# Two row groups for the distance products, and convolution products that leave their result channel by channel

## The chip, the cores and the metric

The kernel runs on one core of one Trainium2 chip. The metric is the device time of one execution in microseconds. The engines are named as the profile names them: PE (TensorE matmul), PEld (TensorE weight load), DVE (VectorE), ACT (ScalarE), POOL (GpSimd), SP (SyncE, which here only issues DMAs).

## The reference, cut to what matters

64 graphs of 256 nodes with 256 features go through two layers, all in float32. The first layer has two branches that meet in a GRU cell. One is a convolution over the nodes, a 1x1 and then a 17-tap one, both with batch norm. The other sends messages weighted by exp(-distance) times the adjacency matrix, with distances between nodes in a learned space of 3 dimensions.

```
xc = transpose(x)                                   # channels by nodes
h = relu(bn1(conv1d(xc, conv1_w)))
h = bn2(conv1d(h, conv2_w, pad 8))                  # 17 taps
x_conv = transpose(relu(h + xc))
s = x @ w_se.T + b_se                               # 3 coordinates per node
sq = sum(s * s)
dist = sq[n] + sq[m] - 2 * (s @ s.T)
A = exp(-dist) * adj
x_nmp = A @ relu(x @ w_msg.T + b_msg)
gi = concat(x_conv, x_nmp) @ w_ih.T + b_ih ; gh = x @ w_hh.T + b_hh
r, z = sigmoid(gi_r + gh_r), sigmoid(gi_z + gh_z)
x1 = layernorm(x + (1 - z) * tanh(gi_n + r * gh_n) + z * x)
# layer 2
h = layernorm(x1)
x2 = layernorm(x1 + x1 + relu((adj @ h) @ W_rel + b_rel + h @ W_root))
```

## The kernel before, in words

The program is one written-out stream: the order in which the Python code issues instructions is the order on each of the five engine queues (`manual_schedule`), and each engine takes its queue in order. PE writes to PSUM, which is a pool of eight banks of 512 columns; every `bank(...)` call takes one, and the matmul that fills it waits for the last reader of the bank's former owner.

**The convolution** handles 8 graphs at a time (`BG`, 8 batches). The 256 nodes of a graph are cut into 16 residues of 16 places, so that the 17-tap filter becomes products of polynomials, which are split by butterflies on DVE into small leaves (`split_all`, `split_u`), multiplied on PE leaf by leaf (`products`, `last_products`, `product`) with 47 matrices of 256x256, and merged back on DVE (`merges` and the statements after `STAGE[b] = "inverse"`). All of it lives in one big tile `X` of 48 slots of 128 x 256; DVE's `stt` helper (L102) does most of the work. In a slot the partitions are channels and the 256 columns are two halves of channels times 128 places. `product` takes 128 columns of a slot as the stationary operand and 256 columns of a matrix as the moving one. So the result comes out with the places on the partitions and the output channels along the columns. The matrices of batch 0 are built in place (`W2[0]`); for later batches they are read from DRAM (`w2m`) into `w`.

After the merges the convolution adds the input x (`x_by_tiles`, loaded as `xb` in four pieces of 512 KB, a pool of two buffers that the next batch's first loads use as well) and turns the sum back to channels by places with PE transposes (`channels`, into `ps_xc`); ACT takes them to SBUF through a Relu into `xc`. The shift of the second batch norm is added along the rows in `last_products` (L419), from `bn2_row`, which `along_rows` makes at the start. The input turned to channels is also written to DRAM once per batch (`xt_dram`, in `conv`) and read back as `xT` by `load`.

**The graphs** go one by one through messages (`messages`), the turning of their 3 coordinates plus half a squared norm (`factors`: two transposes of 128 x 4 into `ps_sT`, two ACT copies into `lr`), the distances (`distances`: two matmuls with 4 rows each, both halves in one bank, then two Exp), the adjacency mask, the message sum (`passing`), the gates (`gates_rz`, `gates_n`), the update, and the second layer (`transposes_h`, `project`, `aggregate`). The loop over k mixes stages of graphs k-1 to k+3. Between the stages stand ten calls of `pump` per graph, which issue the next batch's convolution piece by piece: `conv` is a generator that yields an estimated cost after each piece, and a pump draws pieces until the share of the total that is due has been issued, or until the generator yields None. Batch 0 has no graphs beside it and stands at the start, with the filters.

Of the kernel before, what the change touches and what calls it, by code (L numbers as in the profile page):

```python
# [16 lines left out]
P = 128  # L17
B, N, D = 64, 256, 256
C = D // P
# [30 lines left out]
LEAVES += [(U + 4 + k, U + 6 + k, a) for k, a in enumerate(leaf_angles(PI / 2, 2))]  # L50
LEAVES += [(U + 2, U + 3, PI / 2)]
NM = 3 * len(LEAVES) + 2
OB = 7


# [19 lines left out]
def gnn_two_layers(  # L75
# [35 lines left out]
        eng.dma_start(out=t, in_=src.rearrange("(c p) n -> p c n", p=P))  # L111
        return t

    def x_by_tiles(b, q):

        t = conv_pool.tile([P, 4, D], F32, tag="xb", name="xb")
        nc.sync.dma_start(
            out=t, in_=x[b * BG:(b + 1) * BG].rearrange("g (t j) d -> (g t) j d", j=M)[:, 4 * q:4 * q + 4, :])
        return t


    chan_sb = const.tile([P, 8, C], F32)
    nc.scalar.dma_start(out=chan_sb, in_=chan)
# [12 lines left out]


    bn_scale, bn_shift = [], []
    bn2_row = const.tile([P, 2, D], F32)

    def batch_norms():
        for i in range(2):
# [10 lines left out]

    def along_rows(pool):

        for i, v in enumerate((bn_scale[1], bn_shift[1])):
            ps = bank("ps_row")
            for c in range(C):
                dg = pool.tile([P, P], F32, tag="dg", name="dg", bufs=4)
                nc.vector.tensor_scalar(dg, ident, v[:, c:c + 1], None, ALU.mult)  # L160
                nc.tensor.matmul(ps[:, c * P:(c + 1) * P], ones, dg, start=True, stop=True)
            nc.scalar.copy(bn2_row[:, i, :], ps[:, :D])


    w2m = tc.dram_tile([NM, C, P, D], F32, name="w2m")
# [2 lines left out]
    def filters(pool):  # L168
        W2[0] = pool.tile([P, C, NM, D], F32, name="w2all")
        pieces, groups = [], []  # L170
        for c in range(C):
            for o0, o1 in ((0, 12 * OB), (12 * OB, 24 * OB), (24 * OB, D)):
                starts = [min(o, D - OB) for o in range(o0, o1, OB)]
                for a in range(0, len(starts), 4):
                    groups.append((len(pieces), starts[a:a + 4]))
                pieces.append((c, o0, o1))
        WT = {}

        def fetch(i):
            if i < len(pieces):  # L180
                c, o0, o1 = pieces[i]
                WT[i] = pool.tile([P, TAPS, o1 - o0], F32, tag="wt", name="wt", bufs=2)
                nc.sync.dma_start(out=WT[i], in_=w2T[c, :, :, o0:o1])

        def scaled(i, starts):

            c, o0, o1 = pieces[i]
            ws = pool.tile([P, 4, TAPS, OB], F32, tag="ws", name="ws", bufs=3)
            n, o = len(starts), starts[0]
            nc.vector.tensor_mul(  # L190
                ws[:, :n], WT[i][:, :, o - o0:o - o0 + n * OB].rearrange("p k (b o) -> p b k o", o=OB),
                bn2_row[:, 0, o:o + n * OB].rearrange("p (b o) -> p b o", o=OB).unsqueeze(2)
                .to_broadcast([P, n, TAPS, OB]))
            return ws

        def turned(ws, n):
            ps = bank("ps_tT")
            for b in range(n):
                nc.tensor.transpose(ps[:TAPS * OB, b * P:(b + 1) * P], ws[:, b].rearrange("p k o -> p (k o)"), ident)
            tT = pool.tile([TAPS * OB, 4, P], F32, tag="tT", name="tT", bufs=2)  # L200
            nc.scalar.copy(tT[:, :n].rearrange("k b p -> k (b p)"), ps[:TAPS * OB, :n * P])
            return tT

        fetch(0)
        fetch(1)
        yield
        along_rows(pool)
        TT = {}
        WS = {0: scaled(*groups[0]), 1: scaled(*groups[1])}
        TT[0] = turned(WS[0], 4)  # L210
        for i, (piece, starts) in enumerate(groups):
            c = pieces[piece][0]
            if i + 2 < len(groups):
                WS[i + 2] = scaled(*groups[i + 2])
                if groups[i + 2][0] != groups[i + 1][0]:
                    fetch(groups[i + 2][0] + 1)
            if i + 1 < len(groups):
                TT[i + 1] = turned(WS[i + 1], len(groups[i + 1][1]))
            for a, o in enumerate(starts):
                ps = bank("ps_w")  # L220
                nc.tensor.matmul(ps[:, :NM * OB], TT[i][:, a, :], tap_sb, start=True, stop=True)
                skip = OB - D % OB if o == D - OB else 0
                pv = ps[:, :NM * OB].rearrange("p (f o) -> p f o", o=OB)
                nc.scalar.copy(W2[0][:, c, :, o + skip:o + OB], pv[:, :, skip:])
            if i + 1 == len(groups) or pieces[groups[i + 1][0]][0] != c:
                for f in range(0, NM, 8):
                    g = min(f + 8, NM)
                    nc.sync.dma_start(out=w2m[f:g, c].rearrange("f p o -> p f o"), in_=W2[0][:, c, f:g, :])
            yield
# [148 lines left out]
        return lambda m, c: t[:, m, c, :]  # L378

    def product(ps, slot, w, m):  # L380
        for c in range(C):
            nc.tensor.matmul(ps, X[:, slot, c * P:(c + 1) * P], w(m, c), start=(c == 0), stop=(c == C - 1))  # L382

    def products(b, first, sums):

# [16 lines left out]
    def last_products(b):  # L402
# [9 lines left out]

        def take():
            nc.scalar.copy(X[:, S2 + 6, :], p1[:, :D])
            nc.scalar.copy(X[:, U + 1, :], p3[:, D:])
            nc.vector.tensor_sub(X[:, U + 2, :], X[:, S2 + 6, :], p2[:, :D])
            nc.vector.tensor_add(X[:, U + 3, :], X[:, S2 + 6, :], p1[:, D:])

            nc.vector.tensor_add(X[:, U, :], p3[:, :D], bn2_row[:, 1, :])  # L419
        return take  # L420

    def conv(b):
# [97 lines left out]

        xcs = [work.tile([P, C, 4, N], F32, tag="xc", name="xc", bufs=3) for _ in range(2)]

        def channels(q):
            for o in range(C):
                ps = bank("ps_xc")
                for j in range(4):
                    nc.tensor.transpose(ps[:, j * P:(j + 1) * P], X[:, V + 4 * q + j, o * P:(o + 1) * P], ident)
                pv = ps.rearrange("p (j g t) -> p j g t", j=4, g=BG)
                for h in range(2):
                    nc.scalar.activation(  # L530
                        xcs[h][:, o].rearrange("p g (t j) -> p j g t", j=M)[:, 4 * q:4 * q + 4],
                        pv[:, :, 4 * h:4 * h + 4, :], AF.Relu)
                yield 1.0

        before = []
        for q in range(4):
            xb = x_by_tiles(b, q)
            nc.vector.tensor_add(sl(V + 4 * q, 4), sl(V + 4 * q, 4), xb)
            yield cost(4)
            yield None  # L540
            before.append(channels(q))
            if len(before) > 2:
                yield from before.pop(0)
        for c_ in before:
            yield None
            yield from c_
        for g in range(BG):
            XC[b * BG + g] = (xcs[g // 4], g % 4)

# [16 lines left out]

    def messages(k):
        MSG[k] = work.tile([P, C, D], F32, tag="msg", name="msg", bufs=3)
        st = work.tile([P, C, 4], F32, tag="st", name="st", bufs=3)
        for m in range(C):  # L570
            ps = bank("ps_msg")
            for c in range(C):
                nc.tensor.matmul(ps[:, :D + 4], XT[k][:, c, m * P:(m + 1) * P], wms[:, c, :],  # L573
                                 start=(c == 0), stop=(c == C - 1))
            nc.vector.tensor_add(st[:, m, 0:3], ps[:, D:D + 3], bse_row)
            nc.vector.tensor_add(MSG[k][:, m, :], ps[:, :D], bmsg)  # L576
        nc.scalar.activation(MSG[k], MSG[k], AF.Relu)  # L577

# [2 lines left out]
        nc.gpsimd.tensor_mul(sq, st[:, :, 0:3], st[:, :, 0:3])  # L581
        nc.gpsimd.tensor_add(ns, sq[:, :, 0], sq[:, :, 1])
        nc.gpsimd.tensor_add(ns, ns, sq[:, :, 2])
        nc.gpsimd.tensor_scalar(st[:, :, 3], ns, -0.5, None, ALU.mult)
        nc.gpsimd.tensor_scalar(ns, ns, -1.0, None, ALU.mult)
        ST[k] = (st, ns)

    def factors(k):
        st, ns = ST[k]
        ps = bank("ps_sT")  # L590
        for m in range(C):
            nc.tensor.transpose(ps[:4, m * P:(m + 1) * P], st[:, m, :], ident)
        lr = work.tile([4, 2, N], F32, tag="lr", name="lr", bufs=1)
        nc.scalar.activation(lr[:, 0, :], ps[:4, :N], AF.Identity, bias=lone[:, 1:2], scale=lone[:, 0:1])
        nc.scalar.copy(lr[:, 1, :], ps[:4, :N])
        ST[k] = (lr, ns)

    def distances(k):
        lr, ns = ST[k]
        AT[k] = work.tile([P, C, N], F32, tag="AT", name="AT")  # L600
        ps = bank("ps_dist")
        for m in range(C):
            nc.tensor.matmul(ps[:, m * N:(m + 1) * N], lr[:, 0, m * P:(m + 1) * P], lr[:, 1, :], start=True, stop=True)  # L603
        for m in range(C):
            nc.scalar.activation(AT[k][:, m, :], ps[:, m * N:(m + 1) * N], AF.Exp, bias=ns[:, m:m + 1], scale=2.0)

    def mask(k):
        nc.vector.tensor_mul(AT[k], AT[k], ADJ[k])
# [138 lines left out]
    with tc.tile_pool(name="first", bufs=1) as first_pool:  # L747
# [3 lines left out]
        batch_norms()  # L751


        lone = const.tile([4, 2], F32)
        ab = np.zeros((4, 2), np.float32)
        ab[:3, 0] = 1.0
        ab[3, 1] = 1.0
        nc.sync.dma_start(out=lone, in_=nc.inline_tensor(ab, name="last_row_one").ap())

        wms = const.tile([P, C, D + 4], F32)  # L760
        nc.vector.memset(wms[:, :, D + 3:], 0.0)
# [160 lines left out]
```

## Time and profile before

| | |
|---|---|
| median of 10 runs | 2329.11 us (2327.7 to 2332.95) |
| the profiled execution | 2329.08 us, of which the span of instructions is 2327.3 |
| granted TensorE clock, mean | 0.989 |
| PE busy | 2246.3 us, 97% |
| PEld busy | 1476.6 us, 63% |
| DVE busy | 1685.5 us, 72% |
| ACT busy | 767.3 us, 33% |
| POOL busy | 464.1 us, 20% |
| `ps_k` matmuls (L382) | 297.3 + 41.0 us busy |
| `ps_dist` matmuls (L603) | 74.0 us busy |
| `ps_xc` transposes (L527) | 33.2 us busy |

Busy times of PE and PEld overlap each other. In rows of instruction groups, "x1316" counts hardware passes: each float32 matmul has two records of PE and two weight loads, each transpose one. Mean durations are from issue to end, and passes overlap, so a duration is longer than the step from one pass to the next. In the rows of slices each digit is the busy share, in tenths, of one of 40 equal slices of the span. "<-" after an idle time names what ended it. The windows row lists, for a stretch, its length, then the busy time of PE, PEld, DVE, ACT and POOL, then the granted clock, the share of the DMA engines and GB/s.

### The profile page before, as it was taken

How to read it: one execution, taken by the hardware profiler on the slowest of the kernel's cores; microseconds unless marked ns; L12 is line 12 of the kernel's file. 1: busy time of each engine (PE TensorE's matmuls, PEld its weight loads, DVE VectorE, ACT ScalarE, POOL GpSimd, SP SyncE). 2: the span in 40 equal slices, each digit the busy share in tenths (PEclk: the TensorE clock that was granted, in tenths of full speed). 3: DMA queues.
4: the chain of work that ended last, by engine and by line, in shares of the span. 5: the costliest groups of instructions: out<-in, count | busy, mean ns of one | idle time of the engine just before them, and what ended most of it. 6: DMA issues, size and time to landing. Idle time of an engine off the chain costs nothing.

```text
span 2327.3 us, 24209 instructions
## 1 busy us (share of the span) xinstructions
PE 2246.3 (97%) x8262; PEld 1476.6 (63%) x8262; DVE 1685.5 (72%) x3212; ACT 767.3 (33%) x1577; POOL 464.1 (20%) x922
## 2 busy tenths in 40 slices
PE   7779999999999999999999999999999999999996
PEld 4565676666766676666766566666666666666663
DVE  3893988659794788839886597947889298874443
ACT  4514322442224322342224432243223532243332
POOL 1000321212122212202212221222222122121211
PEclk9989999999999999999999999999999999999998
DMA  6543252223323144221522333231432214321100
GB/s 176 161 154 113 68 168 69 86 85 127 118 77 104 50 136 131 73 100 47 168 89 73 100 127 127 73 109 51 136 119 85 100 37 155 108 78 36 46 23 14
DMA packets 211088, 226.66 MB, mean 97 GB/s; under 512 B 22047, under 2 KB 201750, under 8 KB 210966
## 3 DMA queue, kind: packets, MB, share of 16 engines
q1 hardware_dynamic: 188408, 191.14, 25.7%
q10 hardware_dynamic: 22558, 33.99, 4.1%
q8 instruction: 66, 1.08, 0.2%
q14 instruction: 56, 0.46, 0.1%
HBM read 179.22 MB, written 45.88 MB: 97 GB/s over the span
## 4 chain that ended last, share of the span: by engine, by line
PE 77%; DVE 16%; DMA 3%; issue 2%; POOL 1%; ACT 1%; ACTq 0%; SPq 0%; POOLq 0%; DVEq 0%
PE ps_rz L633 16%; PE ps_k L382 11%; PE ps_n L645 8%; PE ps_rz L631 8%; PE ps_out L708 7%; DVE XF L102 5%; PE ps_c L453 5%; PE ps_nmp L615 5%; PE ps_n L643 4%; PE ps_out L720 4%; PE ps_msg L573 4%; PE ps_dist L603 2%; DVE w L102 2%; DVE bst L650 1%; DMA w<-w2m 1%
## 5 line engine op out<-in xcount | busy, mean ns | idle before, releaser
L102 DVE SCALAR_TENSOR_TENSOR XF<-XF 128x512 f32<-128x512 f32 (+2 forms) x800 | 506.7, 664 | 7.0
L672 POOL TENSOR_SCALAR q<-mv 128x2 f32<-128x2 f32 x64 | 32.1, 501 | 1478.0 <-DVE mv L651 1478.0
L382 PE MATMUL ps_k<-w,XF 128*128 128x256 f32 x1316 | 297.3, 382 | 4.3 <-DMA w<-w2m 1.7
L382 PEld LDWEIGHTS ps_k<-w,XF 128*128 128x128 f32 x1316 | 247.1, 190 | 49.8 <-PE ps_n L645 6.1
L646 DVE TENSOR_TENSOR gn<-ps_n,brzn 128x512 f32<-128x512 f32 x128 | 88.1, 688 | 247.5 <-PE ps_n L645 247.5
L637 ACT ACTIVATE rz<-rz 128x512 f32<-128x512 f32 x128 | 80.6, 630 | 513.8 <-DVE rz L636 513.8
L631 PE MATMUL ps_rz<-whh,xT 128*128 128x512 f32 x512 | 240.8, 593 | 0.0
L633 PE MATMUL ps_rz<-wih,xc 128*128 128x512 f32 x512 | 240.7, 592 | 0.0
L633 PE MATMUL ps_rz<-wih,nmp 128*128 128x512 f32 x512 | 240.6, 592 | 0.0
L708 PE MATMUL ps_out<-wrr,hT 128*128 128x512 f32 x512 | 232.3, 597 | 5.7 <-ACT hT L697 5.7
L636 DVE TENSOR_TENSOR rz<-ps_rz,brzn 128x512 f32<-128x512 f32 x128 | 87.6, 684 | 196.8 <-PE ps_rz L633 196.8
L633 PEld LDWEIGHTS ps_rz<-wih,nmp 128*128 128x128 f32 x512 | 97.4, 190 | 122.3 <-issue 122.3
L633 PEld LDWEIGHTS ps_rz<-wih,xc 128*128 128x128 f32 x512 | 97.4, 190 | 122.3 <-issue 121.3
L708 PEld LDWEIGHTS ps_out<-wrr,hT 128*128 128x128 f32 x512 | 98.1, 192 | 104.8 <-issue 92.4
L573 PE MATMUL ps_msg<-wms,xT 128*128 128x260 f32 x512 | 135.7, 406 | 18.9 <-DVE XF L398 11.0
L577 ACT ACTIVATE msg<-msg 128x512 f32<-128x512 f32 x64 | 40.3, 630 | 343.5 <-DVE msg L576 343.5
L631 PEld LDWEIGHTS ps_rz<-whh,xT 128*128 128x128 f32 x512 | 92.4, 191 | 64.4 <-issue 61.1
L643 PE MATMUL ps_n<-whh,xT 128*128 128x256 f32 x512 | 131.6, 380 | 0.0
L645 PE MATMUL ps_n<-wih,xc 128*128 128x256 f32 x512 | 131.5, 379 | 0.0
L645 PE MATMUL ps_n<-wih,nmp 128*128 128x256 f32 x512 | 131.5, 379 | 0.0
L573 PEld LDWEIGHTS ps_msg<-wms,xT 128*128 128x128 f32 x512 | 95.1, 195 | 52.9 <-issue 23.8
L709 ACT COPY hr<-ps_out 128x256 f32<-128x256 f32 x128 | 47.6, 372 | 242.0 <-PE ps_out L708 242.0
(104 smaller groups left out, 3625.7 us busy)
## 6 DMA issues: line engine op xcount, KB each, us to landing
w<-w2m SPq DMA_DIRECT2D x105, 768.0 KB, 6.0
xn<-in_x_dram SPq DMA_DIRECT2D x32, 512.0 KB, 4.4
xt<-xTc ACTq DMA_DIRECT2D x32, 512.0 KB, 3.3
xT<-xt SPq DMA_DIRECT2D x64, 256.0 KB, 3.0
adj<-in_adjT_dram SPq DMA_DIRECT2D x64, 256.0 KB, 2.8
x<-in_x_dram SPq DMA_DIRECT2D x64, 256.0 KB, 3.0
xb<-in_x_dram SPq DMA_DIRECT2D x32, 512.0 KB, 4.8
out_dram<-y ACTq DMA_DIRECT2D x64, 256.0 KB, 2.2
```

The lines of the kernel that those rows point to most:

```text
L102: nc.vector.scalar_tensor_tensor(o, in0, s, in1, op0=op0, op1=op1)
L382: nc.tensor.matmul(ps, X[:, slot, c * P:(c + 1) * P], w(m, c), start=(c == 0), stop=(c == C - 1))
L453: nc.tensor.matmul(ps, w1[:, c, o * P:(o + 1) * P], xTc[:, c, :], start=(c == 0), stop=(c == C - 1))
L573: nc.tensor.matmul(ps[:, :D + 4], XT[k][:, c, m * P:(m + 1) * P], wms[:, c, :], start=(c == 0), stop=(c == C - 1))
L615: nc.tensor.matmul(ps[:, d * N:(d + 1) * N], MSG[k][:, m, d * P:(d + 1) * P], AT[k][:, m, :], start=(m == 0), stop=(m == C - 1))
L631: nc.tensor.matmul(prz, XT[k][:, c, q], whh[:, c, 0:2 * D], start=(c == 0), stop=False)
L633: nc.tensor.matmul(prz, t, wih[:, i, 0:2 * D], start=False, stop=(i == 3))
L643: nc.tensor.matmul(pn[:, D:], XT[k][:, c, q], whh[:, c, 2 * D:], start=(c == 0), stop=(c == C - 1))
L645: nc.tensor.matmul(pn[:, :D], t, wih[:, i, 2 * D:], start=(i == 0), stop=(i == 3))
L646: nc.vector.tensor_add(RZ[k][1][:, n, :], pn, brzn[:, 2 * D:])
L708: nc.tensor.matmul(ps, hT[:, c, n * P:(n + 1) * P], wrr[:, c, :], start=(c == 0), stop=(c == C - 1))
L720: nc.tensor.matmul(po, ADJ[k][:, m, n * P:(n + 1) * P], hr[:, m, :], start=False, stop=(m == C - 1), skip_group_check=True)
```

## The change

Four things change together.

- `product` takes the 128x128 quarters of a matrix as the stationary operand and 128 columns of the slot as the moving one. The result then has the output channels on the partitions. A product is four matmuls with 128 moving columns instead of two with 256.
- With that, the back transposes are gone. `add_x` adds the input from `xt_dram`, pair of graphs by pair of graphs, in place of `x_by_tiles`; `channels` is two ACT Relus per pair straight from `X`, with the second batch norm's shift as a bias. The shift along the rows is no longer made or added.
- The tile `st` of coordinates holds them twice, at columns 0 to 3 and 32 to 35, in three constant tiles that are zeroed once. `factors` turns 36 columns instead of 4, so that the turned coordinates lie on partitions 0 to 3 and again on 32 to 35.
- `distances` takes its first half from the first copy and its second half from the second, and writes each half to a bank of its own.

The generator yields less than before in its last part: no pause (None) stands between the additions any more, and the transposes' cost is gone from the total by which pumps are paced.

The diff, cut to its core:

```diff
 def along_rows(pool):
-        for i, v in enumerate((bn_scale[1], bn_shift[1])):
...
+        ps = bank("ps_row")
...
 def product(ps, slot, w, m):
-        for c in range(C):
-            nc.tensor.matmul(ps, X[:, slot, c * P:(c + 1) * P], w(m, c), start=(c == 0), stop=(c == C - 1))
+        for o in range(C):
+            q = slice(o * P, (o + 1) * P)
+            for c in range(C):
+                nc.tensor.matmul(ps[:, q], w(m, c)[:, q], X[:, slot, c * P:(c + 1) * P],
+                                 start=(c == 0), stop=(c == C - 1))
 # last_products, take()
-            nc.scalar.copy(X[:, U + 1, :], p3[:, D:])
+            nc.scalar.copy(X[:, U:U + 2, :].rearrange("p s e -> p (s e)"), p3)
-            nc.vector.tensor_add(X[:, U, :], p3[:, :D], bn2_row[:, 1, :])
 # conv, after the merges
-        def channels(q):
-            for o in range(C):
-                ps = bank("ps_xc")
-                for j in range(4):
-                    nc.tensor.transpose(ps[:, j * P:(j + 1) * P], X[:, V + 4 * q + j, o * P:(o + 1) * P], ident)
...
-                yield 1.0
-        before = []
-        for q in range(4):
-            xb = x_by_tiles(b, q)
-            nc.vector.tensor_add(sl(V + 4 * q, 4), sl(V + 4 * q, 4), xb)
-            yield cost(4)
-            yield None
-            before.append(channels(q))
...
+        view = X[:, V:V + M].rearrange("p j (c r t) -> p j c (r t)", c=C, r=BG)
+        def add_x(pair):
+            xb = conv_pool.tile([P, C, 2 * N], F32, tag="xb", name="xb")
+            nc.sync.dma_start(out=xb, in_=xt_dram[b * BG // 2 + pair])
+            v = view[:, :, :, pair * 2 * M:(pair + 1) * 2 * M]
+            nc.vector.tensor_add(v, v, xb.rearrange("p c (r j) -> p j c r", j=M))
+            yield cost(4)
+        def channels(pair):
+            h, g = pair // 2, 2 * (pair % 2)
+            for o in range(C):
+                nc.scalar.activation(
+                    xcs[h][:, o, g:g + 2].rearrange("p g (t j) -> p j g t", j=M),
+                    view[:, :, o, pair * 2 * M:(pair + 1) * 2 * M].rearrange("p j (g t) -> p j g t", g=2),
+                    AF.Relu, bias=bn_shift[1][:, o:o + 1])
+        for pair in range(BG // 2):
+            yield from add_x(pair)
+            channels(pair)
 # messages (SR = 32, ROWS = 36)
+        twice = st.rearrange("p m (r e) -> p m r e", e=SR)
-            nc.vector.tensor_add(st[:, m, 0:3], ps[:, D:D + 3], bse_row)
+            nc.vector.tensor_add(twice[:, m, :, 0:3], ps[:, D:D + 3].unsqueeze(1).to_broadcast([P, 2, 3]),
+                                 bse_row.unsqueeze(1).to_broadcast([P, 2, 3]))
 # factors
-            nc.tensor.transpose(ps[:4, m * P:(m + 1) * P], st[:, m, :], ident)
+            nc.tensor.transpose(ps[:ROWS, m * P:(m + 1) * P], st[:, m, :ROWS], ident)
 # distances
-        ps = bank("ps_dist")
+        pss = [bank("ps_dist") for _ in range(C)]
         for m in range(C):
-            nc.tensor.matmul(ps[:, m * N:(m + 1) * N], lr[:, 0, m * P:(m + 1) * P], lr[:, 1, :], start=True, stop=True)
+            r = slice(m * SR, m * SR + 4)
+            nc.tensor.matmul(pss[m][:, :N], lr[r, 0, m * P:(m + 1) * P], lr[r, 1, :], start=True, stop=True)
```

More of the change, by code (lines that the diff above doesn't have):

```diff
@@ L52 @@
 NM = 3 * len(LEAVES) + 2
+SR, ROWS = 32, 36
 OB = 7
@@ L112, in weight @@
         return t
[L114 to L119, printed above, removed]
     chan_sb = const.tile([P, 8, C], F32)
@@ L138, in gnn_two_layers @@
     bn_scale, bn_shift = [], []
-    bn2_row = const.tile([P, 2, D], F32)
+    bn2_row = const.tile([P, D], F32)
     def batch_norms():
@@ L154, in along_rows @@
     def along_rows(pool):
-        for i, v in enumerate((bn_scale[1], bn_shift[1])):
-            ps = bank("ps_row")
-            for c in range(C):
[L159 to L162, printed above, removed]
+        ps = bank("ps_row")
+        for c in range(C):
+            dg = pool.tile([P, P], F32, tag="dg", name="dg", bufs=2)
+            nc.vector.tensor_scalar(dg, ident, bn_scale[1][:, c:c + 1], None, ALU.mult)
+            nc.tensor.matmul(ps[:, c * P:(c + 1) * P], ones, dg, start=True, stop=True)
+        nc.scalar.copy(bn2_row, ps[:, :D])
     w2m = tc.dram_tile([NM, C, P, D], F32, name="w2m")
@@ L191, in scaled @@
                 ws[:, :n], WT[i][:, :, o - o0:o - o0 + n * OB].rearrange("p k (b o) -> p b k o", o=OB),
-                bn2_row[:, 0, o:o + n * OB].rearrange("p (b o) -> p b o", o=OB).unsqueeze(2)
+                bn2_row[:, o:o + n * OB].rearrange("p (b o) -> p b o", o=OB).unsqueeze(2)
                 .to_broadcast([P, n, TAPS, OB]))
@@ L380, in product @@
     def product(ps, slot, w, m):
-        for c in range(C):
-            nc.tensor.matmul(ps, X[:, slot, c * P:(c + 1) * P], w(m, c), start=(c == 0), stop=(c == C - 1))
+        for o in range(C):
+            q = slice(o * P, (o + 1) * P)
+            for c in range(C):
+                nc.tensor.matmul(ps[:, q], w(m, c)[:, q], X[:, slot, c * P:(c + 1) * P],
+                                 start=(c == 0), stop=(c == C - 1))
     def products(b, first, sums):
@@ L521, in conv @@
         xcs = [work.tile([P, C, 4, N], F32, tag="xc", name="xc", bufs=3) for _ in range(2)]
-        def channels(q):
-            for o in range(C):
-                ps = bank("ps_xc")
-                for j in range(4):
[L527 to L532, printed above, removed]
-                yield 1.0
-        before = []
-        for q in range(4):
-            xb = x_by_tiles(b, q)
-            nc.vector.tensor_add(sl(V + 4 * q, 4), sl(V + 4 * q, 4), xb)
-            yield cost(4)
-            yield None
-            before.append(channels(q))
[L542 to L546, printed above, removed]
+        view = X[:, V:V + M].rearrange("p j (c r t) -> p j c (r t)", c=C, r=BG)
[7 more added lines that the diff above has]
+            h, g = pair // 2, 2 * (pair % 2)
+            for o in range(C):
+                nc.scalar.activation(
[5 more added lines that the diff above has]
+            channels(pair)
         for g in range(BG):
@@ L568, in messages @@
         MSG[k] = work.tile([P, C, D], F32, tag="msg", name="msg", bufs=3)
-        st = work.tile([P, C, 4], F32, tag="st", name="st", bufs=3)
+        st = sts[k % len(sts)]
+        twice = st.rearrange("p m (r e) -> p m r e", e=SR)
         for m in range(C):
@@ L583, in messages @@
         nc.gpsimd.tensor_add(ns, ns, sq[:, :, 2])
-        nc.gpsimd.tensor_scalar(st[:, :, 3], ns, -0.5, None, ALU.mult)
+        nc.gpsimd.tensor_scalar(twice[:, :, :, 3], ns.unsqueeze(2).to_broadcast([P, C, 2]), -0.5, None, ALU.mult)
         nc.gpsimd.tensor_scalar(ns, ns, -1.0, None, ALU.mult)
@@ L591, in factors @@
         for m in range(C):
-            nc.tensor.transpose(ps[:4, m * P:(m + 1) * P], st[:, m, :], ident)
-        lr = work.tile([4, 2, N], F32, tag="lr", name="lr", bufs=1)
-        nc.scalar.activation(lr[:, 0, :], ps[:4, :N], AF.Identity, bias=lone[:, 1:2], scale=lone[:, 0:1])
-        nc.scalar.copy(lr[:, 1, :], ps[:4, :N])
+            nc.tensor.transpose(ps[:ROWS, m * P:(m + 1) * P], st[:, m, :ROWS], ident)
+        lr = work.tile([ROWS, 2, N], F32, tag="lr", name="lr", bufs=1)
+        nc.scalar.activation(lr[:, 0, :], ps[:ROWS, :N], AF.Identity, bias=lone[:, 1:2], scale=lone[:, 0:1])
+        nc.scalar.copy(lr[:, 1, :], ps[:ROWS, :N])
         ST[k] = (lr, ns)
@@ L600, in distances @@
         AT[k] = work.tile([P, C, N], F32, tag="AT", name="AT")
-        ps = bank("ps_dist")
+        pss = [bank("ps_dist") for _ in range(C)]
         for m in range(C):
-            nc.tensor.matmul(ps[:, m * N:(m + 1) * N], lr[:, 0, m * P:(m + 1) * P], lr[:, 1, :], start=True, stop=True)
+            r = slice(m * SR, m * SR + 4)
+            nc.tensor.matmul(pss[m][:, :N], lr[r, 0, m * P:(m + 1) * P], lr[r, 1, :], start=True, stop=True)
         for m in range(C):
-            nc.scalar.activation(AT[k][:, m, :], ps[:, m * N:(m + 1) * N], AF.Exp, bias=ns[:, m:m + 1], scale=2.0)
+            nc.scalar.activation(AT[k][:, m, :], pss[m][:, :N], AF.Exp, bias=ns[:, m:m + 1], scale=2.0)
     def mask(k):
@@ L751, in gnn_two_layers @@
         batch_norms()
[L754 to L757, printed above, removed]
+        lone = const.tile([ROWS, 2], F32)
+        ab = np.zeros((ROWS, 2), np.float32)
+        for r in range(0, ROWS, SR):
+            ab[r:r + 3, 0] = 1.0
+            ab[r + 3, 1] = 1.0
         nc.sync.dma_start(out=lone, in_=nc.inline_tensor(ab, name="last_row_one").ap())
+        sts = [const.tile([P, C, 2 * SR], F32, name=f"st{i}") for i in range(3)]
+        for st in sts:
+            nc.gpsimd.memset(st, 0.0)
         wms = const.tile([P, C, D + 4], F32)
```

## The prediction

> **What bounds the kernel now.** I read the page first: the busy shares, then the slices.
>
> ```profile
> span 2327.3 us, 24209 instructions
> PE 2246.3 (97%) x8262; PEld 1476.6 (63%) x8262; DVE 1685.5 (72%) x3212; ACT 767.3 (33%) x1577; POOL 464.1 (20%) x922
> PE   7779999999999999999999999999999999999996
> DVE  3893988659794788839886597947889298874443
> ```
>
> PE has 81 us of idle time in all. The slices put it at the two ends; in between PE stands at 9 everywhere, also where DVE is at 5. The windows query says how little is left in the middle:
>
> ```profile
> 400.00:2200.00 1800.00, 1786.15 (x6594) 1171.31 (x6592) 1336.64 (x2566) 597.30 (x1227) 392.39 (x768) 1.00 0.29 95
> ```
>
> 13.9 us of 1800 are PE idle, at full clock. So in the steady part **a nanosecond taken from PE's stream is a nanosecond of span**, unless the change opens a new wait. Groups by shape, on PE, give what the three touched streams cost now (count is in passes: an f32 matmul is recorded as two, a transpose as one):
>
> ```profile
> L382 PE MATMUL ps_k<-w,XF 128*128 128x256 f32 x1316 | 297.3, 382 | 4.3 <-DMA w<-w2m 1.7 <-ACT AT L605 1.4 <-DVE XF L299 1.0
> L603 PE MATMUL ps_dist<-lr 4*128 4x256 f32 x256 | 74.0, 409 | 2.9 <-ACT lr L595 2.9
> L382 PE MATMUL ps_k<-w2all,XF 128*128 128x256 f32 x188 | 41.0, 380 | 0.0
> L527 PE MATMUL ps_xc<-ident,XF 128*128 128x128 f32 x256 | 33.2, 273 | 3.5 <-DVE XF L538 3.5
> ```
>
> The mean ns is a latency; passes overlap. What one costs in the stream is the step between starts, and the timeline shows it:
>
> ```profile
> 509.04 1.03 PE L645 MATMUL ps_n<-wih,xc 128*128 128x256 f32 x4
> 509.90 1.03 PE L645 MATMUL ps_n<-wih,nmp 128*128 128x256 f32 x4
> 510.77 0.60 PE L695 MATMUL ps_hT<-ident,h 128*128 128x128 f32 x4
> 511.20 1.88 PE L631 MATMUL ps_rz<-whh,xT 128*128 128x512 f32 x4
> ```
>
> Four passes of 256 columns take 0.86 us (215 ns each), four of 128 take 0.43 (108 ns).
>
> [...]
>
> ```profile
> 1000.69 1.02 PE L708 MATMUL ps_out<-wrr,hT 128*128 128x512 f32 x2
> 1001.64 1.12 PE L603 MATMUL ps_dist<-lr 4*128 4x256 f32 x4
> 1002.70 0.92 PE L573 MATMUL ps_msg<-wms,xT 128*128 128x260 f32 x3
> ```
>
> From the first distance pass to the first message pass is 1.06 us for four passes worth 0.86[...]
>
> ```profile
> 7.14 2.08 PE L161 MATMUL ps_row<-dg,ones 128*128 128x128 f32 x8
> 7.14 1.78 PEld L161 LDWEIGHTS ps_row<-dg,ones 128*128 128x128 f32 x8 [0.39 <-DVE dg L160]
> 1035.59 0.30 PEld L643 LDWEIGHTS ps_n<-whh,xT 128*128 128x128 f32 x2
> ```
>
> The first two are the only f32 matmuls of 128 columns with a load of 128 columns each in this kernel: 8 passes start to start at (2.08-0.42)/7 = 0.237 us (0.42 is one pass), the first one longer[...] two 190 ns loads within 0.30 us, so the second began 0.11 after the first.
>
> **The change, part by part.**
>
> *Turn-back transposes (L523-546).* 8 batches x 32 passes go. In seven batches they lie in the saturated stream: 7 x 32 x 0.109 = **-24.4 us**. With them go 16 ScalarE reads per batch (L530, 626 ns mean); 8 of twice the size come, at an estimated 0.6 to 0.9 us each: at most equal, on an engine 33% busy, so nothing. The four DVE additions per batch stay, same size (L538, 1214 ns), now with a strided second operand: equal to doubled, so 0 to +39 us of DVE in all, at the end of a batch where DVE has its 4s and 5s; I take nothing.[...] per batch one DVE addition (L419, 0.42 us) goes and one copy doubles (L415, 0.37 to 0.58).
>
> *End of batch 0.* Now the gates of the first graph stand behind all four additions and the last eight transposes: PE waits 1.50 us at 188.38 for L538 and starts the gates at 189.28. Afterwards each graph needs its own pair alone. PE would go from passing(0), which starts at 175.17 and takes 3.50, through messages(2), 3.33 us, to the gates at 182.0. That is 7.3 us sooner; the clock there is 0.69 on average[...], so part is given back: **-6** (between -3 and -7.3).
>
> *Loads.* Per batch four 512 KB loads of xb (4.8 us to landing) come from xt instead of x. Same size, same SP queue, same two buffers. But they are now taken without a pause between the additions: by the order of the changed program pairs 0 and 1 come in one pump, 2 and 3 in the next two, where four pumps lay between 65 and 69. The load of pair 2 starts when addition 0 has freed its buffer; between lie addition 1 (1.2) and one gate addition (0.7), so DVE can wait 4.8 - 1.9 = 2.9 us, and ScalarE's Relu of that pair behind it. Queued behind are the gate additions on DVE and hT on ScalarE. PE is in gates_n and gates_rz then, 8 us long, and hT is wanted only at the next project, so this is hidden: 0, at most 7 x 2.9 = +20 if it is not.
>
> *Products (L380-382).* The same multiplications, but 8 passes of 128 columns in place of 4 of 256. 4 x 215.5 = 862 ns against 8 x 108.5 = 868; there are 376 products: **+3** (0 to +9 at 110.5 ns). All count: the start-up products are on the chain too.
>
> *Distances (L598-605).* Two matmuls of two passes each.[...] three steps, not four. 62 graphs in the steady part x 0.215 = **-13.3**. Bounds: nothing saved and the second load no longer hidden, as with the group's first pass (1.12 - 0.374, the usual pass, leaves 0.75 for three steps, so one of 0.32 beside two of 0.215), +0.105 x 62 = +6.5; two steps saved, -26.7. The transposes of 36 instead of 4 columns keep their 128-column pass, the doubled 3-column DVE additions (147 ns) and POOL writes (314 ns)[...]: nothing.
>
> *Banks.* The distances take two of the eight PSUM banks, the transposed channels none. Before, PE waited 11.0 us in 14 places for messages behind DVE L398, and 1.4 for L382 behind the Exp. In the order of the changed program the 14 first places go, and 14 of another kind come: messages (seven with nothing between, seven with four transposes) behind the Exp of the distances. One is worth about 0.37 (end of pass) + 2 x 0.465 (Exp) less 0.3[...] = 1.0 us, or 0.6: 7 x 1.0 + 7 x 0.6 = 11. An even exchange; I add **+3** for waits that PE's earlier arrival opens (0 to +12).
>
> *Start.* One DVE and PE group less in along_rows, three memsets more on POOL: below 1 us, taken as nothing.
>
> **Sum.** -24.4 - 6 + 3 - 13.3 + 3 = -37.7. The profiled execution took 2329.08, the median of the runs is 2329.11, so the same: **2291 us**.
>
> **Rivals.**
> - *The row groups do not overlap* (the second matmul waits for the first): for it, no trace shows an overlap[...]. -24 us: 2305.
> - *Two steps are saved* per graph: -51, 2278.[...]
> - *The waits come out*: loads, Relu and banks are not hidden. +20: 2311. For it: DVE and ScalarE take their queues in order; against it: PE has banks in hand, DVE waits 247.5 us for ps_n.
> - *The weight load becomes the bound of the products*, the slower side. 3008 passes; the rest saves 40.7 us, so it decides from 40.7 / 3008 = 13.5 ns a pass, that is 121 ns instead of 107.5.[...] at the row's 190 ns: 2536. Against it are the two places above.
>
> **Chances.** My sum 0.52 (2283 to 2301), no overlap 0.18, waits 0.15 (of which 0.03 within 0.2% and 0.01 slower), two steps 0.05, load-bound 0.10. Faster by over 0.2% (4.7 us, about what a measurement of this kernel can tell): 0.86, same 0.03, slower 0.11. Range 2276 to 2322: it takes in the first four and leaves out the load-bound products and the far ends.
>
> **What would show it.** PE busy down to about 2205 with idle in 400 to 2200 still below 20 us; ps_k twice the passes, steps of 108 to 110 ns, busy about 340 in all; no ps_xc; ps_dist to ps_msg 0.85 us instead of 1.06; the first gates near 182. Wrong: a ps_k step over 120 ns, ps_dist still at 1.06, PE idle at messages or before project.

## The result, and the profile after

The changed kernel takes **2374.3 us** (median of 9 runs), the kernel before 2330.41 beside it: ratio 1.0187, 95% interval 1.0176 to 1.0198. It is 1.9% slower; forecast was 2291, 1.7% faster. One execution of r5 below, with a granted clock of 0.557 throughout, took 3855.13 us and is left out of its time. The page of the changed kernel, busy shares and slices:

```profile
span 2367.1 us, 26609 instructions
PE 2226.7 (94%) x9506; PEld 1503.9 (64%) x9506; DVE 1704.1 (72%) x3202; ACT 771.2 (33%) x1512; POOL 474.1 (20%) x925
PE   7879999999999999999999999999989999999996
DVE  3895868768784987849778587866878498694543
```

PE is busy for 19.6 us less (about 41 were forecast), and the span is 39.8 us longer: idle time of PE went from 81 to 140 us. The windows query finds it in the middle, where there was little before:

```profile
400.00:2200.00 1800.00, 1731.58 (x7363) 1166.96 (x7362) 1344.52 (x2543) 588.60 (x1149) 397.61 (x752) 0.99 0.29 95
```

68 us idle of 1800 instead of 13.9. The mean granted clock fell from 0.989 to 0.977 as well. The touched groups, by shape:

```profile
L377 PE MATMUL ps_k<-XF,w 128*128 128x128 f32 x2632 | 324.3, 286 | 53.9 <-DVE XF L394 22.9 <-DMA w<-w2m 10.3 <-ACT XF L393 8.4
L597 PE MATMUL ps_dist<-lr 4*128 4x256 f32 x256 | 46.9, 443 | 20.8 <-ACT lr L588 20.8
L377 PE MATMUL ps_k<-XF,w2all 128*128 128x128 f32 x376 | 42.1, 275 | 0.0
```

The transposes are gone and the distances fell from 74.0 to 46.9 us. But the products, which had waited 4.3 us, wait 53.9, and the distances wait 20.8 instead of 2.9.

**Where the products wait.** PE in the second batch of graphs, the timeline of the changed kernel:

```profile
631.78 0.70 PE L597 MATMUL ps_dist<-lr 4*128 4x256 f32 x4
632.41 1.14 PE L565 MATMUL ps_msg<-wms,xT 128*128 128x260 f32 x4
634.14 1.14 PE L565 MATMUL ps_msg<-wms,xT 128*128 128x260 f32 x4 [0.59 <-ACT AT L599]
635.12 1.95 PE L377 MATMUL ps_k<-XF,w 128*128 128x128 f32 x16
640.34 3.84 PE L377 MATMUL ps_k<-XF,w 128*128 128x128 f32 x32 [3.27 <-DVE XF L394]
```

A product group has 48 passes and fills three banks; its first 16 passes go to the first two. Then PE stops: the third bank is still the third bank of the group before, and L394, its reader, comes late. DVE at that time:

```profile
635.16 0.69 DVE L294 TENSOR_TENSOR XF<-XF 128x512 f32<-128x512 f32 x1
635.77 0.68 DVE L657 TENSOR_TENSOR w<-x,nn 128x512 f32<-128x512 f32 x1
636.49 0.69 DVE L103 SCALAR_TENSOR_TENSOR w<-rz,w 128x512 f32<-128x512 f32 x1
...
639.03 0.66 DVE L292 TENSOR_TENSOR XF<-XF 128x512 f32<-128x512 f32 x1
639.61 0.68 DVE L394 TENSOR_TENSOR XF<-XF,ps_k 128x512 f32<-128x512 f32 x1
```

DVE is not idle, it is in the graph's `update` (635.77 to 639), which the program issues ahead of that read. The generator yields between a product and its evacuation, so the evacuation (`take`) is drawn by whichever pump comes next, and here `update` stands between.

**Where the distances wait.** ACT, the same kernel:

```profile
728.80 2.10 ACT L530 ACTIVATE xc<-XF,bnsh 128x512 f32<-128x512 f32 x2
730.71 0.61 ACT L611 COPY nmp<-ps_nmp 128x512 f32<-128x512 f32 x1
731.23 0.55 ACT L587 ACTIVATE lr<-ps_sT,lone 36x256 f32<-36x256 f32 x1
731.69 0.34 ACT L588 COPY lr<-ps_sT 36x256 f32<-36x256 f32 x1
```

Eight Relus (L530, 1.16 us each in the median) stand in ACT's queue from 719 to 731 us, behind additions that wait for their loads, and hold up the copies to `lr`; the distances start at 732.08 after 2.41 us of idle PE.

**The slow clock** comes on top. Messages after such a gap, and after none:

```profile
1010.89 1.23 PE L597 MATMUL ps_dist<-lr 4*128 4x256 f32 x4 [2.90 <-ACT lr L588]
1012.05 2.10 PE L565 MATMUL ps_msg<-wms,xT 128*128 128x260 f32 x4
...
1057.09 0.70 PE L597 MATMUL ps_dist<-lr 4*128 4x256 f32 x4
1057.72 1.14 PE L565 MATMUL ps_msg<-wms,xT 128*128 128x260 f32 x4
```

After 2.90 us of idle PE the same four passes take 2.10 us instead of 1.14: they run at half speed, and the granted clock from 1012 to 1014.1 us is 0.50. Not every gap does this: after the 3.27 us before 640.34 and the 2.41 us before 732.08 the clock stays at 1.00. Added up over windows of 5 us from 300 to 2200 us, the changed kernel loses 29.0 us to the clock, in 14 places of some 1.7 or 3.4 us each; the kernel before loses nothing there.

Theories: **PACING**, that the waits come from where the pumps now draw the pieces of the convolution, since its estimated total fell from 107.7 to 99.7 with the transposes; **BANKS**, that the second bank of the distances is to blame. The runs were to tell what the parts of the change are worth from what the shifted schedule costs.

### The profile page after: what moved, and what is told of

Read it like the earlier page. It is cut to its first block, busy times and chain, and to the rows that moved or that the text cites. A ratio compares the mean times of both kernels' runs of the same rounds, so it can differ in the third digit from the quotient of the medians.

```text
span 2367.1 us, 26609 instructions
## 1 busy us (share of the span) xinstructions
PE 2226.7 (94%) x9506; PEld 1503.9 (64%) x9506; DVE 1704.1 (72%) x3202; ACT 771.2 (33%) x1512; POOL 474.1 (20%) x925
## 4 chain that ended last, share of the span: by engine, by line
PE 74%; DVE 15%; DMA 5%; ACT 2%; issue 2%; POOL 1%; SPq 0%; ACTq 0%; POOLq 0%; DVEq 0%
PE ps_rz L627 15%; PE ps_k L377 14%; PE ps_n L639 8%; PE ps_rz L625 7%; PE ps_out L702 5%; PE ps_c L447 5%; DVE XF L103 4%; PE ps_nmp L609 4%; PE ps_msg L565 4%; PE ps_n L637 4%; PE ps_out L714 4%; DMA w<-w2m 2%; DVE XF L524 2%; DMA xb<-xt 2%; PE ps_dist L597 1%
## 5 line engine op out<-in xcount | busy, mean ns | idle before, releaser
L377 PE MATMUL ps_k<-XF,w 128*128 128x128 f32 x2632 | 324.3, 286 | 53.9 <-DVE XF L394 22.9
L377 PEld LDWEIGHTS ps_k<-XF,w 128*128 128x128 f32 x2632 | 318.0, 201 | 71.1 <-issue 32.2
L666 POOL TENSOR_SCALAR q<-mv 128x2 f32<-128x2 f32 x64 | 38.8, 607 | 1469.2 <-DVE mv L645 1469.2
L565 PE MATMUL ps_msg<-wms,xT 128*128 128x260 f32 x512 | 140.6, 419 | 12.1 <-DMA adj<-in_adjT_dram 8.0
```

What stands on the lines that cost most here:

```text
L377: nc.tensor.matmul(ps[:, q], w(m, c)[:, q], X[:, slot, c * P:(c + 1) * P], start=(c == 0), stop=(c == C - 1))
```

## The experiments

**r1: the end of the convolution paced as before** (changed kernel):

```diff
+                yield 1.0                    # in channels, per Relu
+        before = []
         for pair in range(BG // 2):
             yield from add_x(pair)
-            channels(pair)
+            yield None
+            before.append(channels(pair))
+            if len(before) > 2:
+                yield from before.pop(0)
+        for c_ in before:
+            yield None
+            yield from c_
```

> The changed kernel with the end of the convolution paced as before: a pause after each addition, each pair's Relu two pieces late, 1.0 of cost per Relu, so every pump draws the same pieces as in the kernel before. Theory PACING (the new waits come from where the pumps now put the products and from the bunched additions and Relus): PE idle in 400 to 2200 us falls from 68 to under 25 us, the half-speed stretches of the clock in that part vanish, and the time is about 2330 - 24 (transposes) - 26 (distances, two steps of 0.215 saved) + 13 (products at 112 ns) - 5 = 2288 us. Theory BANKS (the second bank of the distances makes products and messages wait): idle stays above 45 us, time over 2340.

Measured: 2298.35 us, ratio 0.9854 (0.984 to 0.9869). PE idle in 400 to 2200 is 20.2 us (68.4 in the changed kernel, 13.9 before). Of the product waits 3.3 us for DVE and DMA are left, and 11.3 for the Exp. PACING holds; 10 us of the forecast were missing, of which the clock (3.4 us in the windows from 300 to 2200) explains a part.

**r2: only the cost restored**:

```diff
         for pair in range(BG // 2):
             yield from add_x(pair)
             channels(pair)
+        yield 8.0
```

> The changed kernel with only the total cost of the convolution restored (8.0 yielded once at its end): products stand in the same pumps as in the kernel before, the additions and Relus still follow each other without a pause. PACING: the waits of products for DVE L394, ACT L393 and DMA w (some 42 us) vanish, the wait of the distances behind the Relus (ACT lr, 20.8 us) stays; about 2288 + 21 + 8 x 1.7 of slow clock = 2323 us. BANKS: products still wait some 30 us, time over 2340.

Measured: **2290.4 us**, ratio 0.9822 (0.9807 to 0.9836). One yield, with no instruction in it, turns 1.9% slower into 1.8% faster. Page and product groups of r2:

```profile
span 2290.0 us, 26575 instructions
PE 2201.7 (96%) x9506; PEld 1479.0 (65%) x9506; DVE 1702.2 (74%) x3202; ACT 774.1 (34%) x1512; POOL 465.2 (20%) x925
L377 PE MATMUL ps_k<-XF,w 128*128 128x128 f32 x2632 | 308.1, 276 | 14.8 <-ACT AT L600 11.3 <-DVE rz L631 1.6 <-DMA w<-w2m 1.1
L598 PE MATMUL ps_dist<-lr 4*128 4x256 f32 x256 | 45.2, 429 | 3.0 <-ACT lr L589 3.0
```

Between this and the changed kernel lie 77.1 us of span: 52.1 of PE idle (140.4 against 88.3) and 25.0 of PE busy on the same instructions. The latter fits the clock: of the 29.0 us that the changed kernel loses to it between 300 and 2200 us, r2 loses nothing (granted clock 1.00 from 220 to 2260 us). The part of the expectation that the wait for `lr` would stay was wrong: it fell to 3.0 us, though there too no pause stands between the additions. They are merely drawn in other pumps.

**r3: the kernel before with the distances alone changed** (coordinates twice, two row groups, a bank each; the diff's lines for `messages`, `factors` and `distances`).

> The kernel before with only the distances changed (coordinates turned twice, two row groups, a bank each). PACING: two passes of 215 ns saved in 62 graphs, 26 us, with waits as before or a few us more: 2304 us, and the step from the first distance to the first message 0.63 instead of 1.06 us. BANKS: the banks' waits eat it: PE idle in 400 to 2200 over 40 us, time 2330 or more.

Measured: 2315.41 us, ratio 0.9928 (0.9914 to 0.9943), between the two theories' times. The step from the first distance to the first message is 0.63 us (1042.74 to 1043.37), and PE idle in 400 to 2200 is 20.8 us, not over 40. PE busy fell by 24.2 us (2222.1 against 2246.3), idle rose from 81.0 to 93.1. In the waits of PE the messages wait 4.4 us behind products instead of 11.0, and the products 11.6 behind the Exp instead of 1.4: a bank more for the distances moves and adds a little waiting. It does not explain the result.

**r4: the kernel before, its transposes' cost yielded as 0**, no instruction changed but their order:

```diff
-                yield 1.0
+                yield 0.0
```

> The kernel before with the 8.0 of cost of its back transposes yielded as 0, nothing else: the pumps are paced by 99.7 as in the changed kernel, so the products move to its pumps. PACING: the products' waits appear here without any of the change: 20 to 50 us slower, 2350 to 2380 us, PE idle in 400 to 2200 over 35 us. BANKS: no such wait, within 5 us of 2330.

Measured: 2384.99 us, ratio 1.0229 (1.0212 to 1.0246), a little above the 2350 to 2380 expected; PE idle in 400 to 2200 is 39.1 us. Waits of PE in r4:

```profile
PE ps_k L382 <- DVE XF L398: 26.4, 7, 3.8
PE ps_k L382 <- DMA w<-w2m: 19.1, 11, 2.9
```

The stall of the changed kernel, seven times up to 3.8 us, without any of its operations (L398 is the same DVE read). BANKS is out as the cause: this kernel has one bank for the distances.

**r5 and r9: products kept apart**, in the changed kernel with its short cost (r9 is the same kernel once more, for its profile):

```diff
+            if i:
+                yield None
             take = make()
```

> The changed kernel, its shorter cost and its bunched additions kept, with a pause (None) ahead of every product but the first, so that no pump holds the end of one product and the start of the next. Theory ADJACENT (the products' waits come from two products standing in one pump, so that PE meets the second while the first one's evacuation still waits in DVE's and ACT's queues): the waits of ps_k for DVE L394, ACT L393 and DMA w, 42 us in the changed kernel, fall below 12; the wait of the distances for lr stays near 20; time about 2374 - 30 - a third of the slow clock = 2330 us or less. Theory SHARE (the products suffer because the whole convolution is drawn too slowly, not because of neighbours): the waits stay above 30 us and the time stays over 2360.

> The kernel of r5 once more, for a profile at full clock. ADJACENT: time near 2305 us as in r5, the waits of ps_k for DVE L394, ACT L393 and DMA w below 12 us together (42 in the changed kernel), the wait of the distances for lr still near 20. SHARE has no place left at 2305, unless those waits are still there.

Measured: r5 2303.71 us, ratio 0.9877 (0.9861 to 0.9894); r9 2305.08. Waits of PE in r9:

```profile
PE ps_dist L599 <- ACT lr L590: 21.4, 9, 2.8
PE ps_msg L567 <- ACT XF L393: 8.5, 7, 1.2
PE ps_k L377 <- DMA w<-w2m: 2.3, 4, 1.1
```

The products' 42 us are down to 2.3, with the pace of the changed kernel; the wait for `lr` is whole, and the 8.5 us behind ACT's read (L393) now stand at the messages. So the cause is not the slower pace as such.

The picture of ADJACENT, two products in one pump, is not what the timelines show, though. In the changed kernel the products at 620.09 and 635.12 have gates, projection, distances and messages between them. r9 leaves the read (L394) behind `update`, as it was, and only moves the next product on, from behind the messages to behind `aggregate`:

```profile
625.34 5.52 PE L377 MATMUL ps_k<-XF,w 128*128 128x128 f32 x48
626.01 0.68 DVE L394 TENSOR_TENSOR XF<-XF,ps_k 128x512 f32<-128x512 f32 x1
```

The third bank is wanted after 16 passes, at about 627.1, and the read has ended at 626.7. And r2, too, issues a product (629.91) before the one before it (617.58) has been read (636.78), and hardly waits:

```profile
617.58 5.52 PE L377 MATMUL ps_k<-XF,w 128*128 128x128 f32 x48
629.91 1.16 PE L377 MATMUL ps_k<-XF,w 128*128 128x128 f32 x8
631.58 4.73 PE L377 MATMUL ps_k<-XF,w 128*128 128x128 f32 x40 [0.51 <-ACT AT L600]
636.78 0.68 DVE L394 TENSOR_TENSOR XF<-XF,ps_k 128x512 f32<-128x512 f32 x1
637.52 1.15 PE L566 MATMUL ps_msg<-wms,xT 128*128 128x260 f32 x4 [0.33 <-DVE XF L394]
```

Its second product comes ahead of the messages and waits for a bank of the Exp; the bank behind L394 goes to the messages, at 637.52. So the cause is narrower than ADJACENT has it: a product stalls where it meets a bank whose read stands late in the reader's queue, and the pace decides which stage meets that bank.

**r6: pauses between the additions alone**, Relus two pieces late, at no cost (r1 with `yield 0.0`).

> The changed kernel with pauses between the additions and the Relus two pieces late, at no cost: the pacing of the products is that of the changed kernel. PACING: the wait of the distances for lr falls from 20.8 to under 6 us, the products' waits (42 us) stay; about 2374 - 15 - 8 = 2350 us. If the bunching were the main cause: under 2330.

Measured: 2368.55 us, ratio 1.0157 (1.014 to 1.0174). The wait for `lr` fell only to 12.9 us, and the wait for DMA w rose from 10.3 to 18.2; the product waits stayed. Less than expected: the bunching is the smaller part, and spreading it helps little while the rest stands.

**r7: cost restored, distances as before**, so the convolution's part alone.

> The changed kernel with the 8.0 of cost restored and the distances as before (one bank, one row group, 4 columns): the convolution's part alone. With r2 at 2290 and the kernel before at 2331: if the two parts add up without meeting each other, -24 (transposes) -7 (start) +13 (products at 112 ns) gives 2312, and the distances are worth 22 us on top; if the extra bank costs as much as it did in the kernel with row groups alone (16 gained of 26), 2306.

Measured: 2306.68 us, ratio 0.989 (0.9875 to 0.9905). By the ratios of r7 and r2 the distances are worth 16 us on top (0.0068 of 2331); in the kernel before (r3) they were worth 16 too. The parts add up.

**r8, r10, r11: other costs in place of r2's 8.0** (4.0, 11.0, 7.0).

> The changed kernel with 4.0 of cost added at the end of the convolution, half of what was removed. If the time follows the pace smoothly, it lies halfway, near 2332 us. If it hangs on which stages the products meet (ADJACENT), it can lie anywhere between 2290 and 2375, and goes with the ps_k waits: by the order of the program no product directly follows another one's bank here, so under 2310.

> The changed kernel with 11.0 of cost added at the end of the convolution. By the order of the program no product here stands directly behind another one's bank (ps_k3 behind the DVE read of ps_k3, or ps_k2 behind the ACT read of ps_k1): ADJACENT gives 2285 to 2300 us. A smooth dependence on the pace with its best at the old total gives some 2310.

> The changed kernel with 7.0 of cost added: 1.0 less than in r2 (2290 us). By the order of the program 14 third banks of a product come straight behind the DVE read of the product before (none in r2). ADJACENT: 14 waits of 1 to 3.3 us with some slow clock, 2305 to 2340 us. If the time followed the pace smoothly between r8 (4.0: 2294) and r2 (8.0: 2290): 2291.

| cost added | 0 | 4 | 7 | 8 | 11 |
|---|---|---|---|---|---|
| us | 2374.3 | 2294.2 | 2373.85 | 2290.4 | 2295.32 |
| ratio | 1.0187 | 0.9835 | 1.0166 | 0.9822 | 0.9832 |

No smooth curve. r8 and r10 came as expected. From 8.0 to 7.0 the time jumps by some 80 us. In PE's order the product group between distances and messages in r2 stands behind the messages in r11. The timeline of r11:

```profile
647.41 0.70 PE L598 MATMUL ps_dist<-lr 4*128 4x256 f32 x4
648.04 1.15 PE L566 MATMUL ps_msg<-wms,xT 128*128 128x260 f32 x4
649.58 1.15 PE L566 MATMUL ps_msg<-wms,xT 128*128 128x260 f32 x4 [0.40 <-ACT AT L600]
650.57 1.95 PE L377 MATMUL ps_k<-XF,w 128*128 128x128 f32 x16
656.98 3.25 PE L377 MATMUL ps_k<-XF,w 128*128 128x128 f32 x14 [4.46 <-DVE XF L394]
```

It happens twice per batch there; the waits of PE in r11 name 14 places:

```profile
PE ps_k L377 <- DVE XF L394: 60.6, 14, 4.5
```

The 14 places were foreseen from the order of the program, their size was not: 2305 to 2340 us were expected, from waits of 1 to 3.3 us. The waits are up to 4.5 us long, and the 14 passes after the wait shown take 3.25 us, about twice 112 ns each.

r8 and r10 have other waits (15.7 us of products behind DVE in r8, 14.3 behind DMA w in r10), none of this kind, and are near the best.

**r12: r2 with the additions walking x contiguously**, the convolution's tile in steps.

> r2 (cost restored) with the additions walking x contiguously and the convolution's tile in steps, instead of the other way round. The addition takes 1.93 us in the changed kernel against 1.21 before. If only the read of x in steps of 64 bytes is dear: back to about 1.2 us, 32 x 0.7 = 22 us less DVE work; off the critical path mostly, so 2286 to 2290 us. If any step in either operand is dear: 1.9 us or more, and 2290 or above.

Measured: 2293.47 us, ratio 0.9824 (0.9805 to 0.9843): no difference from r2. The addition in r12:

```profile
L525 DVE TENSOR_TENSOR XF<-XF,xb x32: 2007/2061/2141, 177.5 to 2047.3; 128x1024 f32<-128x1024 f32 x32
```

2.06 us against 1.92 in the changed kernel and 1.21 before: steps are dear on either side, and it is off the path.

## Why the prediction was wrong, step by step

**The step that failed is "Banks", with "Loads" beside it**: +3 us were put down for waits (0 to +12), and PE idle grew by 59 us, with 29 us lost to the slow clock on top. The part on banks listed the places behind the Exp, where the messages in the end wait 4.1 us in 7 places, and left out those where a product's bank still belonged to the product before. It priced a place by the length of the read itself (two Exps of 0.465 us), less 0.3 us, the step from the last distance pass to the first message pass in the kernel before (1002.40 to 1002.70), and not by when the reader's queue gets to it: the read stood behind 3.3 us of `update`. That the pumps are paced by a total which the change had shortened was known, and it got no term in the sum. r4 prices it: the pacing alone costs 2.3% without the change.

**"Loads"** had the mechanism but the wrong victim. DVE does wait for the loads, 18.0 us in 16 places. The prediction followed the Relus' delay to hT and the gate additions; it was `lr`, two copies further down ACT's queue, that PE wanted soon (20.8 us). The Relu's price was also too low: 1.16 us in the median, not 0.6 to 0.9, eight of them within 12 us. Whether the bias, which got no term in the sum, or the output in steps makes it dear is not told apart.

**"Distances"** was mis-sized: -13.3 was taken, with -26.7 as the other end. That one step of four would go was the author's estimate, with no trace behind it. The step from the first distance to the first message is now 1057.72 - 1057.09 = 0.63 us, from 1.06: two steps of 0.215 are gone. Busy time fell by 27.1 us. The transposes of 36 columns take 273 ns in the median, as those of 4 did. In r3, where the distances change alone, a third of the gain is given back in waits.

**"Products"** was mis-sized the other way: +3 taken, 0 to +9 allowed. In r2 they are busy 308.1 + 42.1 = 350.2 us against 338.3 before, so +12; in the timeline of r2, 40 passes from 647.96 to 652.43 take 4.47 us, 112 ns each. The rival of a load-bound product asked for over 121 ns, and was rightly held small: it does not explain the slower result. The eight passes at 7.14 us, read as evidence against it, are none by themselves: they step by 0.237 us each, but the transposes just before them, at 5.21 us, step by 0.22, where those at 21.61 step by 0.11. The granted clock does not show it: the profile gives 1.00 from 5 to 22 us.

**"Turn-back transposes"** came out: none are left. **"End of batch 0"** was too small: the first gates start at 178.95 instead of 189.28, 10 us sooner where 6, at most 7.3, were taken, though they then wait 1.73 for `nmp`.

So r2's 2290 beside the forecast of 2291 is partly two errors that cancel (distances 14 too small, products 9 too small), and the sum was right only for a schedule that the change did not keep. Of the rivals, "the waits come out" had the right kind at a quarter of the size: its cap of +20 was one load's wait per batch, and no second, no third place, and no clock.

What stays open: why the clock falls after some gaps and not after others, and where the rest of r1's missing 10 us lies. No run moves `take` itself ahead of `update`, so that the read's late place is seen in the timelines and by r9 and r11, not removed on its own.

## What to carry to other kernels

Where work is interleaved by estimated cost, removing an operation moves everything behind it: keep the old total while a change is measured, then tune the pace as a thing of its own. Before a bank is counted as free, look up what stands ahead of its reader in the reader's own queue, not only how much work lies between on PE. When a saturated PE gets idle gaps of 3 us, price them above their length, since the passes after them may run at half speed (2.10 us for 1.14 after the gap of 2.90 us).

## What the runs showed of the hardware that was not expected

- Two float32 matmuls of 4 rows, two passes each, take 0.63 us to the next matmul with one on rows 0 to 3 and the other on rows 32 to 35, each with its own bank (1057.09 to 1057.72 in the changed kernel, 1042.74 to 1043.37 in r3). Both on rows 0 to 3 and in one bank they took 1.06 (1001.64 to 1002.70 in the kernel before): two of four steps of 0.215 us are gone.
- 128-column float32 passes with a load of 128 columns each run every 112 ns (r2, 40 passes from 647.96 to 652.43 us), transposes every 108 (the kernel before, four from 510.77 to 511.20 us).
- A float32 addition of 128x1024 takes 1.21 us with plain operands (the kernel before), 1.92 with one operand read in steps of 64 bytes (the changed kernel), 2.06 with the other in steps (r12).
- In the changed kernel a gap of 2.90 us in PE's work was followed by passes at half speed (2.10 us for 1.14, granted clock 0.50 from 1012 to 1014.1 us); gaps of 2.41 and 3.27 us were not (granted clock 1.00 after both).
